# Cross-attention in split fp32r on one core: Q and K side by side, bv prefilled by ScalarE, two SBUF pools, a new order

## The chip, the cores and the metric

One core of a Trainium2 chip. The metric is the device time of one execution in microseconds (us). An execution's span runs from its first to its last profiled instruction; the time is a little longer than the span.

## The reference

For 8 batches, with x1 and x2 of 512 channels by 1024 positions in fp32 and D = 64:

```python
q = jnp.einsum('bcn,dc->bnd', x1, Wq) + bq
k = jnp.einsum('bcn,dc->bdn', x2, Wk) + bk[:, None]
v = jnp.einsum('bcn,dc->bdn', x2, Wv) + bv[:, None]
attn = jax.nn.softmax(jnp.einsum('bnd,bdm->bnm', q, k), axis=2)
attn_out = jnp.einsum('bcm,bnm->bcn', v, attn)
return attn_out + x1
```

Since the rows of attn sum to one, bv can be added behind the attention; the kernel does so, and writes the output transposed (position by channel).

## The kernel before

**The work of a batch.** Q and K are projected as plain fp32 matmuls of 64 columns (16 instructions each: 4 channel chunks, 2 halves of the positions, each in its own half of TensorE's columns). V, the scores and the output are products of fp32 operands, each split into a high part, a low part and a difference, and multiplied in three fp32r passes. The first two passes are accumulated in a PSUM bank, ScalarE scales the bank, and the third pass is added.

- V: 8 units j of 128 positions. VX(j) is the high and the low pass (4 matmuls each), vf(j) the scaling, VY(j) the third pass; vh, vl and vd split the result, ready for the output. The x2 chunks are split by xh (ScalarE), xl and xd (VectorE), one chunk for two units. In batch 0 units 0 and 1 are done by plain fp32 matmuls instead (VF).
- Scores: S(h, i), 2 matmuls for one half h of the rows and one block i of 128 columns; Sc copies them out of PSUM. Softmax goes by quarters Q of the rows: F and T find the maximum (T by GpSimd across partitions), and then by units u of 128 rows: L subtracts it (VectorE), E is exp (ScalarE), H, l and d make the three parts eh, el and ed (ScalarE, VectorE, VectorE). es, a1, a2, a3 and tot make the sum of a quarter (ScalarE, a DMA that accumulates, VectorE twice, GpSimd), few moves it by two small DMAs, rec inverts it.
- Output: R(u, m) is the high and low pass of unit u over block m of V, 2 matmuls; fx(u) scales the bank; D(u, m) is the third pass, 1 matmul. lo(u) fills an output tile with bv by a broadcast DMA from DRAM, oa(u) adds x1T to it by a DMA that accumulates (issued by GpSimd), ev(u) adds the attention (VectorE), st(u) stores it. Unit 7 of the last batch is added and stored in two halves, ev/st and ew/sw.
- Q and K: Q and K are the matmuls, qe and ke take them out of PSUM with the bias (ScalarE, two instructions), qd and kc copy each half to the other 64 partitions by two DMAs, qr and kr make the high parts (ScalarE), ql and kl the low ones (VectorE).

**The order** is written out by hand: three strings of words, FIRST for batch 0, MIDDLE for batches 1 to 6, LAST for batch 7. A word names a method and its arguments; a + ahead of it means the next batch, a - the one before. follow (line 481) calls them one by one, and each engine executes its own instructions in that order, each waiting for its operands and for a free buffer. SyncE's queue holds the loads, lo, st, few, qd and kc, in that order too. In MIDDLE the next batch's Q and K are separated by other matmuls, and the loads of x1 stand ahead of Q, those of x2 between the two:

```python
VY.5 vl.2 H.3 vf.3 vh.5 a2.0 a3.0 vh.4 vl.4 VY.3 vf.6 +ldx1.0 +Q vl.5 vh.3 T.2 l.3 F.3 VY.6 VX.7 tot.0 +qe R.0.0
...
H.4 l.4 +K E.5 es.2 vh.7 vl.7 R.0.7 +qd R.1.7 oa.1 +qr l.2 +ql vd.3 +ke fx.1 R.4.0 R.3.6 R.3.7 few.0 fx.3 R.4.1
```

In FIRST, batch 0's own K and Q follow one another on TensorE.

**Buffers.** Tiles of one tag rotate through as many buffers as BUFS gives it (one where it says nothing); a new tile waits until the tile that had the buffer is no longer read. kh, kl and kd hold both the parts of x2 (xh, xl, xd) and those of the exponentials (H, l, d); x holds the loads of x1 and x2; o the output tiles. q and k of a batch share one buffer (tag qk). In PSUM, tag B (5 banks) holds the units of V and of the output, tag sc (3 banks) Q, K and the scores.

Of the kernel before, what the change touches and what calls it, by code (L numbers as in the profile page):

```python
# [9 lines left out]
F32 = mybir.dt.float32  # L10
# [4 lines left out]

# [3 lines left out]

FIRST = """  # L30
VF.0.0 VF.0.1 VF.1.0 VF.1.1 ldx2.0 lwq VF.0.2 ldx2.1 wh.0 wl.0 VF.1.2 wd.0 VF.1.3 wh.1 ldx1.0 w4.0 wl.1 xh.1
w4.1 VF.0.3 vf.0 xl.1 VX.2 vh.0 vf.1 xh.3 vh.1 K ldx1.1 ke kc lo.0 vf.2 wd.1 Q xh.2 vl.0 qe xl.3 xd.1 VY.2 vh.2
xl.2 VX.4 xd.3 vl.1 qd VX.5 vd.0 kr vf.4 vf.5 qr kl VX.3 +ldx1.0 vf.3 xd.2 VY.4 vh.4 VY.5 lo.1 ql vl.2 VY.3
S.0.2 vh.5 S.0.0 vh.3 S.0.5 S.0.1 vl.4 S.0.3 vl.5 Sc.0.2 S.1.5 S.0.4 vd.2 Sc.0.0 Sc.0.5 Sc.0.1 Sc.0.3 S.0.6 vl.3
S.0.7 S.1.7 Sc.0.4 S.1.0 Sc.0.6 Sc.0.7 +ldx1.1 F.0 S.1.6 S.1.1 Sc.1.1 oa.1 VX.7 T.0 vd.1 L.0 Sc.1.5 vf.7 Sc.1.7
E.0 L.1 +Q E.1 VX.6 F.1 T.1 VY.7 S.1.3 H.0 l.0 Sc.1.0 R.0.0 S.1.2 Sc.1.6 es.0 H.1 S.1.4 Sc.1.3 +ldx2.0 L.2 +qe
vf.6 R.0.1 R.0.2 L.3 R.0.3 R.0.4 vh.7 +ldx2.1 VY.6 Sc.1.2 Sc.1.4 a1.0 l.1 R.1.0 R.1.1 R.1.2 E.3 d.0 R.1.3 R.1.4
R.1.5 R.0.5 F.2 vl.7 vh.6 H.3 +K l.3 R.3.0 T.2 d.1 vl.6 a2.0 +qd R.0.6 R.1.6 oa.0 E.2 R.3.1 R.3.2 R.3.3 R.3.4
R.3.5 R.3.6 R.0.7 H.2 l.2 +qr L.4 es.1 R.2.0 R.2.1 R.2.2 R.2.3 R.2.4 fx.0 a1.1 E.4 F.3 H.4 D.0.0 R.3.7 a3.0
R.2.5 d.3 R.2.6 R.2.7 l.4 fx.3 D.3.0 R.1.7 R.4.0 T.3 lo.3 D.0.1 D.0.2 fx.2 +ql L.6 E.6 lo.2 D.3.1 D.3.2 D.3.3  # L40
D.3.4 D.3.5 R.4.1 R.4.2 +ke a2.1 d.2 R.4.3 R.4.4 R.4.5 tot.0 vd.3 few.0 R.4.6 L.5 fx.1 D.0.3 D.0.4 D.2.0 D.0.5
D.0.6 H.6 D.2.1 D.2.2 D.0.7 +kc l.6 +xh.0 rec.0 E.5 R.4.7 a3.1 D.1.0 D.1.1 D.1.2 D.1.3 D.1.4 D.1.5 D.1.6 D.2.3
es.2 oa.2 H.5 ev.0 L.7 fx.4 E.7 d.4 st.0 D.1.7 R.6.0 D.2.4 D.3.6 tot.1 ev.1 R.6.1 R.6.2 R.6.3 R.6.4 R.6.5 R.6.6
+kr l.5 a1.2 +xl.0 R.5.0 D.2.5 D.4.0 R.5.1 D.3.7 R.6.7 D.2.6 few.1 H.7 +xh.1 R.5.2 R.5.3 D.4.1 d.6 es.3 oa.3
R.5.4 +kl +S.0.7 d.5 fx.6 +Sc.0.7 +S.0.5 R.5.5 D.2.7 st.1 D.6.0 +S.0.6 +Sc.0.5 a2.2 +xh.3 a3.2 +Sc.0.6 +S.0.3
a1.3 +S.0.2 R.5.6 lo.4 +Sc.0.3 +Sc.0.2 rec.1 ev.2 st.2 ev.3 st.3 +S.0.0 R.5.7 +S.0.1 l.7 D.4.2 +Sc.0.0 +xl.1
D.6.1 D.4.3 +S.0.4 +xd.0 tot.2 +VX.1 D.4.4 +Sc.0.4 +vf.1 +Sc.0.1 D.6.2 few.2 a2.3 lo.5 +F.0 a3.3 D.6.3 +S.1.6
lo.7 D.4.5 +Sc.1.6 rec.2 D.4.6 D.4.7 oa.4 d.7 +VX.0 ev.4 fx.5 D.5.0 D.5.1 D.6.4 D.6.5 +S.1.3 +vf.0 +VY.0 D.6.6
D.5.2 D.5.3 D.6.7 +xh.2 +T.0 R.7.0 lo.6 +L.1 +xl.3 R.7.1 tot.3 few.3 +L.0 +xd.1 oa.6 +F.1 rec.3 +Sc.1.3 oa.5
+E.1 +S.1.4 +H.1 oa.7 R.7.2 R.7.3 R.7.4 R.7.5 R.7.6 st.4 R.7.7 fx.7 +VY.1 D.7.0 D.7.1 D.7.2 +S.1.5 ev.6 +vh.1  # L50
+Sc.1.4 +xl.2 +E.0 D.7.3 D.7.4 D.7.5 D.5.4 D.5.5 D.5.6 D.5.7 ev.5 +vh.0
"""
# [40 lines left out]
def kernel(  # L93
# [41 lines left out]
    def new(shape, tag, name, dtype=F32):  # L135
        return sb.tile(shape, dtype, tag=tag, name=name, bufs=BUFS.get(tag, 1))

# [355 lines left out]


_OUT = (8, 1024, 512)


# [26 lines left out]
```

## Time and profile before

| | |
|---|---|
| Median of 3 runs | 655.53 us (655.47 to 656.39) |
| The profiled execution, its time | 656.37 us |
| its span | 654.6 us |
| TensorE busy | 648.5 us |
| VectorE busy | 563.3 us |
| ScalarE busy | 400.2 us |
| GpSimd busy | 195.3 us |
| Bytes moved by DMA | 106.73 MB, 163 GB/s in the mean |

Engines are named as the profile names them: PE is TensorE's matmuls, PEld its weight loads, DVE VectorE, ACT ScalarE, POOL GpSimd, SP SyncE; a q behind the name means its instruction queue, as where it issues a DMA. L418 is line 418 of the kernel. A row of a group reads: line, engine, operation, output<-inputs, shapes, xcount | busy us, mean ns of one | idle time of the engine just ahead of them, and what ended most of it. Matmuls are pipelined: one's duration is longer than the distance to the next one's start, and the distance is what it costs.

### The profile page before, as it was taken

The page shows a single profiled execution, that of the slowest core. Times are in us where ns is not written, and L with a number is a line of the kernel's source. Part 1 is how long each engine was busy: PE and PEld are TensorE (multiplying, and loading weights), DVE is VectorE, ACT ScalarE, POOL GpSimd, SP SyncE. Part 2 cuts the span into 40 slices and gives each one's busy share as a digit, 9 for nine tenths or more (in the row PEclk, how much of TensorE's full clock was granted, in tenths as well). Part 3 has the DMA queues.
Part 4 walks back from the last instruction along what each step waited for, and adds up shares of the span by engine and source line. Part 5 has one row for each costly group of instructions (what it writes and reads, how often), then busy time and mean ns, then how long its engine had stood idle before and what let it go on. Part 6 is the DMA issues. An engine that isn't in the chain of part 4 may idle for free.

```text
span 654.6 us, 7991 instructions
## 1 busy us (share of the span) xinstructions
PE 648.5 (99%) x2817; PEld 495.3 (76%) x2817; DVE 563.3 (86%) x661; ACT 400.2 (61%) x565; POOL 195.3 (30%) x164
## 2 busy tenths in 40 slices
PE   9999999999999999999999999999999999999997
PEld 4666788668886688866888668886688767888886
DVE  4789989997988979798897988979888798899982
ACT  5786857576466764767547674467645676467530
POOL 0023232324313333134231332313323133322513
PEclk9999999999999999999999999999999999999999
DMA  8645467594565855758557576676747676465466
GB/s 325 211 145 124 88 169 183 205 222 115 103 208 191 189 120 111 215 187 171 135 140 196 192 144 143 154 185 200 138 129 170 168 227 126 117 145 125 76 167 161
DMA packets 50552, 106.73 MB, mean 163 GB/s; under 512 B 14160, under 2 KB 14928, under 8 KB 46800
## 3 DMA queue, kind: packets, MB, share of 16 engines
q1 hardware_dynamic: 35968, 72.14, 34.6%
q0 software_dynamic: 13824, 33.56, 29.4%
q10 hardware_dynamic: 720, 0.53, 0.2%
q8 instruction: 22, 0.36, 0.2%
q14 instruction: 18, 0.15, 0.1%
HBM read 68.42 MB, written 16.78 MB: 130 GB/s over the span
## 4 chain that ended last, share of the span: by engine, by line
PE 86%; DMA 1%; DVE 1%; issue 0%; ACT 0%; DVEq 0%
PE ps_o L418 49%; PE ps_v L379 22%; PE ps_s L262 8%; PE ps_q L205 3%; PE ps_k L205 3%; DMA x<-in_x_dram 1%; DVE o L447 0%; DVE e L290 0%; DVE el L301 0%; ACT vh L401 0%; ACT ps_v L390 0%; DVEq L520 0%; DVE es L319 0%; DVE ed L306 0%
## 5 line engine op out<-in xcount | busy, mean ns | idle before, releaser
L418 PE MATMUL ps_o<-vh,eh 128*128 128x512 f32 x512 | 200.2, 391 | 0.0
L418 PE MATMUL ps_o<-vl,el 128*128 128x512 f32 x512 | 199.4, 390 | 0.3 <-DVE el L301 0.3
L418 PE MATMUL ps_o<-vd,ed 128*128 128x512 f32 x512 | 139.2, 389 | 0.0
L418 PEld LDWEIGHTS ps_o<-vh,eh 128*128 128x128 f32 x512 | 96.1, 188 | 25.9 <-issue 5.7
L418 PEld LDWEIGHTS ps_o<-vl,el 128*128 128x128 f32 x512 | 96.2, 188 | 20.4 <-DVE el L301 0.7
L418 PEld LDWEIGHTS ps_o<-vd,ed 128*128 128x128 f32 x512 | 96.0, 188 | 20.1 <-ACT ps_o L430 0.2
L329 POOL PARTITION_ALL_REDUCE den<-es x32 | 72.4, 2263 | 105.6 <-DVE es L319 94.1
L267 ACT COPY e<-ps_s 128x512 f32<-128x512 f32 x128 | 70.1, 593 | 49.5 <-PE ps_s L262 49.1
L440 POOL DMA_DIRECT2D o<-in_x1T_dram x64 | 58.2, 1006 | 134.7 <-DMA o<-in_bv_dram 53.6
L290 DVE TENSOR_TENSOR e<-e,top 128x1024 f32<-128x1024 f32 x64 | 88.7, 1388 | 7.7 <-POOL top L282 7.7
L282 POOL PARTITION_ALL_REDUCE top<-max x32 | 44.6, 1395 | 154.5 <-DVE max L278 106.3
L297 ACT ACTIVATE eh<-e 128x1024 fp32r<-128x1024 f32 x64 | 67.6, 1057 | 24.3 <-PE ps_o L418 23.7
L301 DVE TENSOR_TENSOR el<-e,eh 128x1024 fp32r<-128x1024 f32 x64 | 79.4, 1241 | 0.5 <-ACT eh L297 0.3
L306 DVE SCALAR_TENSOR_TENSOR ed<-eh,el 128x1024 fp32r<-128x1024 f32 x64 | 78.1, 1229 | 0.3
L293 ACT ACTIVATE e<-e 128x1024 f32<-128x1024 f32 x64 | 66.8, 1053 | 8.0 <-DVE e L290 7.8
L379 PE MATMUL ps_v<-wh,xh 128*128 128x512 f32 x248 | 66.9, 391 | 0.0
L379 PE MATMUL ps_v<-wl,xl 128*128 128x512 f32 x248 | 66.3, 389 | 0.0
L379 PE MATMUL ps_v<-wd,xd 128*128 128x512 f32 x248 | 64.7, 396 | 0.0
L447 DVE SCALAR_TENSOR_TENSOR o<-ps_o,r,o 128x512 f32<-128x512 f32 (+1 forms) x65 | 47.7, 739 | 18.7 <-PE ps_o L418 15.9
L390 ACT ACTIVATE ps_v<-ps_v 128x512 f32<-128x512 f32 x64 | 37.7, 589 | 40.8 <-PE ps_v L379 39.6
L379 PEld LDWEIGHTS ps_v<-wd,xd 128*128 128x128 f32 x248 | 44.9, 188 | 16.7 <-issue 4.9
L401 ACT ACTIVATE vh<-ps_v 128x512 fp32r<-128x512 f32 x64 | 37.5, 596 | 32.5 <-PE ps_v L379 32.2
(45 smaller groups left out, 815.8 us busy)
## 6 DMA issues: line engine op xcount, KB each, us to landing
x<-in_x_dram SPq DMA_DIRECT2D x29, 1024.0 KB, 7.2
o<-in_bv_dram SPq DMA_DIRECT2D x64, 256.0 KB, 4.5
o<-in_x1T_dram POOLq DMA_DIRECT2D x64, 256.0 KB, 4.6
es<-e POOLq DMA_DIRECT2D x32, 512.0 KB, 6.9
out_dram<-o SPq DMA_DIRECT2D x63, 256.0 KB, 4.0
x<-in_x_dram SPq DMA_DIRECT2D x5, 512.0 KB, 8.9
k<-k SPq DMA_DIRECT2D x16, 128.0 KB, 4.4
q<-q SPq DMA_DIRECT2D x16, 128.0 KB, 9.8
```

What stands on the lines that cost most here:

```text
L262: nc.tensor.matmul(ps, k[:, ts(i, P)], self.qa[:, ts(h, H)], start=(z == 0), stop=(z == 1))
L267: nc.scalar.copy(self.half[h][:, :, i, :], self.ps[h, i].rearrange("p (q n) -> p q n", q=2))
L290: nc.vector.tensor_tensor(e, e, top, ALU.subtract)
L293: nc.scalar.activation(self.unit(u), self.unit(u), AF.Exp)
L297: nc.scalar.activation(self.e[u]["h"], self.unit(u), AF.Copy, scale=SPLIT)
L301: nc.vector.tensor_tensor(self.e[u]["l"], self.unit(u), f32(self.e[u]["h"]), ALU.subtract)
L306: nc.vector.scalar_tensor_tensor(e["d"], f32(e["h"]), -1.0 / T, f32(e["l"]), ALU.mult, ALU.add)
L329: nc.gpsimd.partition_all_reduce(self.den[Q], self.es[Q][:, 0, :], P, ReduceOp.add)
L379: nc.tensor.matmul(self.B[j], self.c[j // 2][z][:, c, ts(j % 2, P)], w[z][:, c, :], start=(start and c == 0), stop=(stop and c == CT - 1), ...
L418: nc.tensor.matmul(self.B[u], self.e[u][z][:, m, :], self.v[m // 2, z][:, m % 2, :], start=start, stop=stop, skip_group_check=True,)
L440: nc.gpsimd.dma_start(self.o[u], x1T[self.b, ts(u, P), :], accum_op=ALU.add)
L447: nc.vector.scalar_tensor_tensor(o, self.B[u][:, at], self.share(u), o, ALU.mult, ALU.add)
```

## The change

- The words of the three orders are rearranged throughout. The next batch's Q and K follow one another on TensorE, with all four loads of x ahead of them, and x has 4 buffers instead of 2.
- VX is divided into XH and XL, two words that can stand apart.
- lo is a copy by ScalarE from bv_sb, a tile that is loaded once by one broadcast DMA (lbv).
- kh, kl, kd and o have one buffer less each. A second SBUF pool, side, holds the tags named in SIDE.
- At the start: the first piece of x2 is issued by SyncE instead of ScalarE, the bias load by SyncE later (lbq), and there are 8 warm-up matmuls instead of 9.
- At the end: the last unit in the order is unit 5. The halves of unit 7 remain, and sw is issued by ScalarE's queue.

The code, and of the orders the lines around Q and K in MIDDLE and the end of LAST:

```diff
 MIDDLE = """
...
+VY.7 vl.4 +ldx2.1 vf.3 -st.7 +Q +qe +K lo.2 L.7 E.7 l.1 H.0 F.2 vh.7 VY.3 VY.6 tot.0 a2.1 vh.3 l.0 vl.3 R.2.0
+R.0.0 vl.7 R.2.1 T.2 L.4 R.2.2 R.2.3 R.1.0 R.1.1 R.2.4 L.5 R.0.1 R.1.2 vd.0 R.2.5 lo.1 +qd +qr vh.6 R.3.0 R.3.1
+a3.1 few.0 lo.0 vl.6 E.5 +ql oa.2 E.4 +ke d.1 es.2 R.0.2 R.2.6 R.2.7 fx.2 R.3.2 R.3.3 R.3.4 R.0.3 R.0.4 d.2 vd.1
...
 LAST = """
...
+L.5 oa.0 -st.7 E.5 fx.0 d.0 R.3.5 R.2.5 L.4 a1.3 R.2.6 R.2.7 H.1 fx.2 oa.2 R.3.6 vd.2 R.3.7 E.4 D.0.0 es.2 D.2.0
...
+D.4.6 oa.5 d.6 D.4.7 oa.6 fx.6 D.6.0 D.6.1 ev.4 st.4 D.6.2 D.6.3 D.6.4 D.6.5 D.6.6 D.6.7 D.5.0 D.5.1 D.5.2 D.5.3
+ev.6 st.6 D.5.4 D.5.5 D.5.6 D.5.7 ev.5 st.5
 """
...
+    side = ctx.enter_context(tc.tile_pool(name="side", bufs=1))
...
+    bv_sb = const.tile([P, C], F32, name="bv_sb")
...
-    BUFS = {"B": 5, "sc": 3, "raw": 2, "top": 2, "kh": 5, "kl": 5, "kd": 4, "es": 2, "few": 2, "r": 2, "o": 4, "x": 2}
+    BUFS = {"B": 5, "sc": 3, "raw": 2, "top": 2, "kh": 4, "kl": 4, "kd": 3, "es": 2, "few": 2, "r": 2, "o": 3, "x": 4}
...
+    SIDE = {"raw", "o", "es", "qk", "fold", "top", "den", "few", "r"}
...
-        return sb.tile(shape, dtype, tag=tag, name=name, bufs=BUFS.get(tag, 1))
+        pool = side if tag in SIDE else sb
+        return pool.tile(shape, dtype, tag=tag, name=name, bufs=BUFS.get(tag, 1))
...
-            nc.scalar.dma_start(self.x2[0][:, 0, c, :], x2[0, :, 0, c])
+            queue = nc.scalar if c else nc.sync
+            queue.dma_start(self.x2[0][:, 0, c, :], x2[0, :, 0, c])
...
+        def lbq(self):
+            nc.sync.dma_start(bqk_sb, bqk)
+
+        def lbv(self):
+            nc.sync.dma_start(bv_sb, bv.broadcast_to([P, C]))
...
-        def VX(self, j):
+        def XH(self, j):
             self.B[j] = bank("B", f"ps_v_{self.b}_{j}")
             self.vpass(j, "h", True, False)
+
+        def XL(self, j):
             self.vpass(j, "l", False, True)
...
-            nc.sync.dma_start(self.o[u], bv.broadcast_to([P, C]))
+            nc.scalar.copy(self.o[u], bv_sb)
...
-            nc.sync.dma_start(outT[self.b, ts(u, P), right], self.o[u][:, right])
+            nc.scalar.dma_start(outT[self.b, ts(u, P), right], self.o[u][:, right])
...
-        nc.scalar.dma_start(bqk_sb, bqk)
...
-        for i, times in enumerate((3, 3, 3)):
+        for i, times in enumerate((3, 3, 2)):
```

103 lines of the change are left out of this document (49 added, 54 removed).

## The prediction

> **What bounds the kernel now.** I read the page of the profile first, then the busy time by stretches, then the waits. Three rows of the page, and two stretches of 80 us out of the middle:
>
> ```profile
> span 654.6 us, 7991 instructions
> PE 648.5 (99%) x2817; PEld 495.3 (76%) x2817; DVE 563.3 (86%) x661; ACT 400.2 (61%) x565; POOL 195.3 (30%) x164
> PE 86%; DMA 1%; DVE 1%; issue 0%; ACT 0%; DVEq 0%
> ```
>
> ```profile
> 180.00:260.00 80.00, 80.00 (x352) 61.70 (x352) 69.81 (x83) 49.39 (x70) 24.46 (x20) 1.00 0.64 163
> 260.00:340.00 80.00, 80.00 (x352) 61.69 (x352) 69.80 (x83) 49.38 (x70) 24.41 (x20) 1.00 0.66 165
> ```
>
> The columns after the stretch are the busy time of PE, PEld, DVE, ACT and POOL, the granted clock and the DMA share. TensorE is busy all of each 80 us, at full clock, and the chain that ended last runs through it. The change removes no matmul outside the warm-up: both orders hold the same projections, scores and outputs. So it can save only what TensorE loses between matmuls, and what lies ahead of its first and behind its last one. It can cost whatever makes TensorE wait. VectorE has about 10 us to spare in 80, ScalarE 30.
>
> What is lost between matmuls inside a batch is seen in TensorE's own timeline around a K projection in the middle, and around K and Q of the first batch, where they already stand side by side:
>
> ```profile
> 298.19 0.39 PE L418 MATMUL ps_o<-vh,eh 128*128 128x512 f32 x1
> 298.41 0.39 PE L418 MATMUL ps_o<-vl,el 128*128 128x512 f32 x1
> 298.73 3.65 PE L205 MATMUL ps_k<-x,wqk_sb 128*64 128x512 f32 x16
> 302.31 0.50 PE L418 MATMUL ps_o<-vh,eh 128*128 128x512 f32 x1
> 302.65 0.40 PE L418 MATMUL ps_o<-vl,el 128*128 128x512 f32 x1
> 302.89 0.39 PE L418 MATMUL ps_o<-vh,eh 128*128 128x512 f32 x1
> ```
>
> ```profile
> 14.19 3.65 PE L205 MATMUL ps_k<-x,wqk_sb 128*64 128x512 f32 x16
> ...
> 17.68 3.60 PE L205 MATMUL ps_q<-x,wqk_sb 128*64 128x512 f32 x16
> ...
> 21.21 1.20 PE L379 MATMUL ps_v<-wd,xd 128*128 128x512 f32 x4
> ```
>
> Durations overlap, so I read starts. Ordinary matmuls start every 0.22 to 0.23 us (298.19 to 298.41). Into the K block it takes 0.32 (298.41 to 298.73), 0.09 too much; behind it 0.34 (302.31 to 302.65), 0.11 too much. The block alone takes 3.58 (298.73 to 302.31); the joined pair of the first batch takes 14.19 to 21.21, 7.02, or 3.51 each, so a lone block loses 0.07 inside as well. Two lone blocks against one joined pair: one entry and one exit less, 0.20, and 7.16 less 7.02, 0.14. That is **0.34 us a batch**.
>
> The waits that reach TensorE, in the list of waits (total, times, longest):
>
> ```profile
> PEld ps_q L205 <- DMA x<-in_x_dram: 1.4, 1, 1.4
> PE ps_q L205 <- DMA x<-in_x_dram: 1.0, 1, 1.0
> PEld ps_v L372 <- DMA x<-in_x_dram: 0.8, 2, 0.5
> PEld ps_o L418 <- DVE el L301: 0.7, 1, 0.7
> PE ps_o L418 <- DVE el L301: 0.3, 1, 0.3
> ```
>
> Once each, in the first 125 us: a Q that waits 1.0 for its load, 0.3 to 0.7 for an el, 0.8 in two pieces for the first loads.
>
> **The change, part by part.**
>
> *Q and K side by side.* Batches 1 to 7 are projected in lone blocks, batch 0 already jointly: 7 x 0.34 = **-2.4 us**. Only the diff's word order is needed for this (+Q +qe +K, with nothing of TensorE between). Their inputs need four x buffers at once instead of two. In a middle batch the four loads now stand at its head; the buffers they take were last read by the previous pair and by xl.3 early in this batch, so they leave some 14 us ahead of Q, by the count of matmuls between. The 1.0 us wait of Q in batch 1 goes the same way, since in the first batch two loads find fresh buffers: **-1.0**.
>
> *bv by ScalarE.*
>
> ```profile
> o<-in_bv_dram SPq DMA_DIRECT2D x40, 256.0 KB, 4.7
> q<-q SPq DMA_DIRECT2D x10, 128.0 KB, 9.9
> k<-k SPq DMA_DIRECT2D x10, 128.0 KB, 4.5
> ```
>
> ```profile
> L312 ACT COPY es<-e 128x1024 f32<-128x1024 f32 x32 | 33.5, 1047 | 0.7
> L390 ACT ACTIVATE ps_v<-ps_v 128x512 f32<-128x512 f32 x64 | 37.7, 589 | 40.8 <-PE ps_v L379 39.6 <-ACT e L267 0.8 <-PE ps_v L372 0.4
> ```
>
> The first fence is the transfers issued from 180 to 580 us (times, size, median to landing). 64 broadcasts of 256 KB leave the SP queue, one of 256 KB (lbv) comes; TensorE waited for none, so I cost the removal at 0. ScalarE gets 64 copies of 128x512 from SBUF to SBUF, which no row shows. Bounds: 0.52 us, half the 1047 ns of the copy twice as wide, and 1.05, all of it; I take 0.6, the row of equal width (589). That is 8 x 0.6 = 4.8 us a batch, on 49.4 busy of 80; hidden in ScalarE's idle time, but each copy stands in order ahead of others. It also waits there for the store that frees its buffer (3 instead of 4); I follow the tightest place below.
>
> *Fewer split buffers (kh, kl, kd each one less) and the new order.* I followed each reuse in a middle batch by counting matmuls at 0.227. Most are free well before, and two places are thin, both behind Q and K. First, ScalarE does qe, lo.2, E.7, H.0 and VectorE l.0, from the end of Q. The durations are in these rows:
>
> ```profile
> L297 ACT ACTIVATE eh<-e 128x1024 fp32r<-128x1024 f32 x64 | 67.6, 1057 | 24.3 <-PE ps_o L418 23.7
> L293 ACT ACTIVATE e<-e 128x1024 f32<-128x1024 f32 x64 | 66.8, 1053 | 8.0 <-DVE e L290 7.8
> L301 DVE TENSOR_TENSOR el<-e,eh 128x1024 fp32r<-128x1024 f32 x64 | 79.4, 1241 | 0.5 <-ACT eh L297 0.3
> L290 DVE TENSOR_TENSOR e<-e,top 128x1024 f32<-128x1024 f32 x64 | 88.7, 1388 | 7.7 <-POOL top L282 7.7
> L405 DVE SCALAR_TENSOR_TENSOR vl<-vh,ps_v 128x512 fp32r<-128x512 f32 x64 | 42.5, 682 | 12.8 <-ACT vh L401 12.5
> L409 DVE TENSOR_TENSOR vd<-vh,vl 128x1024 fp32r<-128x1024 f32 x32 | 39.0, 1219 | 0.3
> L319 DVE TENSOR_TENSOR es<-es 128x256 f32<-128x256 f32 x32 | 13.3, 417 | 0.3
> L212 ACT ACTIVATE q<-ps_q,bqk_sb 64x512 f32<-64x512 f32 x16 | 11.0, 684 | 16.2 <-PE ps_q L205 16.0
> ```
>
> 1.37 + 0.6 + 1.05 + 1.06 + 1.24 = 5.3, and I allow 0.2 for hand-overs. TensorE asks for l.0 after K (3.5), VY.3 and VY.6 (8 matmuls) and 3 more: 6.0. It fits by 0.5. Behind l.0 VectorE does vl.3, vl.7, L.4, L.5, vd.0, a3.1, vl.6: 0.68 + 0.68 + 1.39 + 1.39 + 1.22 + 0.42 + 0.68 = 6.5, so vl.6 is there at 12.0; TensorE asks for it in R.2.6, 37 matmuls behind K, at 3.5 + 8.4 = 11.9. So this just misses, by 0.1: 6 middle batches, **+0.6**. In the last batch ScalarE does E.5, fx.0, H.1 and then fx.2, 1.05 + 0.6 + 1.06 + 0.6 = 3.3, behind an L.5 that VectorE, full until then, ends about 2.8 us ahead of the first D.2: **+0.5**. The wait for el in the first batch (0.3 to 0.7) belongs to an order that is gone; I take **-0.5**.
>
> *The start.*
>
> ```profile
> 0.98 4.02 PE L473 MATMUL ps_warm<-warm 128*128 128x512 bf16 x9 [0.98 <-DVE spark L468]
> ...
> 4.80 7.62 PE L372 MATMUL ps_v<-w_raw,x 128*128 128x512 f32 x16
> ```
>
> One warm-up matmul less would end them 0.4 earlier (9 of them from 0.98 to 4.80), but the first weights now stand second in the SP queue, behind hx.0, so the first VF may start as late as now. VF goes through the chunks in the order of landing, two products on each, which lets the 0.8 of waits go. Bounds 0 and 1.2; I take **-0.4**. The bias load moves from ScalarE's queue to SP's, behind ldx2.1 and ahead of x1; it is asked for by ke, behind K, and moves x1 by 1 KB.
>
> *The end.*
>
> ```profile
> 650.78 0.88 DVE L447 SCALAR_TENSOR_TENSOR o<-ps_o,r,o 128x256 f32<-128x256 f32 x2 [0.92 <-PE ps_o L418]
> 651.72 0.38 SPq L460 DMA_DIRECT2D out_dram<-o  x1
> ```
>
> ```profile
> out_dram<-o SPq DMA_DIRECT2D x3, 256.0 KB, 2.3
> out_dram<-o SPq DMA_DIRECT2D x2, 128.0 KB, 1.8
> L447 DVE SCALAR_TENSOR_TENSOR o<-ps_o,r,o 128x512 f32<-128x512 f32 x63 | 46.8, 747 | 17.8 <-PE ps_o L418 14.9 <-DMA o<-in_x1T_dram 1.8
> ```
>
> Now unit 7 comes last, in two halves: 0.88 of VectorE, then a store of 128 KB that lands in 1.8. The new order ends with unit 5, whole: 0.75, then 256 KB in 2.3. That is 0.5 - 0.13, **+0.4**. The halves of unit 7 and sw.7 on ScalarE's queue are some 14 us from the end. [...]
>
> **Sum:** -2.4 - 1.0 - 0.5 - 0.4 + 0.4 + 0.6 + 0.5 = -2.8. The profiled execution took 656.37 (span 654.6 and 1.8 around it), so 653.6; the median of the runs shown is 655.53, 0.84 less, so **652.7**. Without the two new waits and with all of the start it would be 650.8.
>
> **Rivals.**
>
> *The gains are eaten by thin chains.* If a bv copy takes 1.05 instead of 0.6, H.0, l.0 and vl.6 are each 0.45 later, and R.2.6 waits 0.55: 6 x 0.45 = 2.7 more, 655.4, no change. For it: no row shows the copy, and the chain has no slack. Against it: ScalarE's rows go by width, 589 at 512 and 1047 at 1024.
>
> *Slower: the copy of q holds up the v of unit 6.* In the new order qr, which waits for q's two copies, stands ahead of vh.6 on ScalarE; vl.6, and R.2.6, wait for that. From the end of Q: qe 1.37, copy, qr 1.06, vh.6 0.6, vl.6 0.68. With the 4.5 of k's copy it comes to 8.2 against the 11.9 at which R.2.6 asks; with the 9.9 that q's takes now, to 13.6, 1.7 too late, in 6 batches 10.2: 662.9. It decides from a copy of 8.2 us on. For it: 9.9 is the median now. Against it: now two loads of 1 MB are issued right ahead of q's copy, on the same queue; in the new order the loads stand a third of a batch earlier unless xl.3 or a store's wait on SP holds the last one back.
>
> *It doesn't do what it says:* Q and K adjacent in the order, but K waiting for x2 or for its bank. The bank was read out by Sc.1.6 long before; a late load of a microsecond in each batch would cost 7 x 1.0, 659.7.
>
> **How the numbers follow.** A measurement of this kernel can tell about 0.2%, 1.3 us, from no change. My forecast (650.6 to 654.2) gets 0.62, the thin chains 0.20, q's copy 0.12, a late load or a place that I didn't count 0.06. Faster 0.64 (the forecast and a little of the thin chains), same 0.17, slower 0.19. The range takes in the forecast and the thin chains, 0.82: 650.6 to 657.0.
>
> **What would show it.** In the timeline a period between Q blocks of about 79.9 to 80.0 instead of 80.2, with ps_q and ps_k adjacent; no wait of ps_q for x; ACT copies of o from bv_sb at about 600 ns; q's copy landing in under 6 us; the last store whole. If TensorE shows waits for vl or el in every batch, a thin chain decides; if ScalarE's qa waits more than 2 us for q, the second rival. I am wrong if the period is longer than 80.2.

## The result and the profile after

| | before | after |
|---|---|---|
| Median of 4 runs each | 655.78 us (655.47 to 656.39) | 660.10 us (659.38 to 661.46) |
| Ratio | | 1.0067 (95% interval 1.0049 to 1.0085) |
| The profiled execution, its time | 656.37 us | 661.46 us |
| its span | 654.6 us | 659.7 us |

The change made the kernel slower by 0.67%, where 652.7 us was forecast. Of the six executions of the run e8 below, two lie over 1.5% above its fastest one and are left out of its median, range and ratio. The page of the profile after, the same two stretches of 80 us as before, and TensorE's timeline around one joined pair:

```profile
span 659.7 us, 8029 instructions
...
PE 650.4 (99%) x2816; PEld 496.3 (75%) x2816; DVE 557.0 (84%) x661; ACT 433.8 (66%) x629; POOL 198.6 (30%) x164
```

```profile
180.00:260.00 80.00, 79.78 (x350) 61.13 (x349) 68.03 (x81) 52.74 (x77) 23.76 (x21) 1.00 0.57 139
260.00:340.00 80.00, 80.00 (x354) 62.18 (x353) 70.84 (x85) 53.65 (x79) 25.01 (x21) 1.00 0.55 138
```

```profile
205.74 1.07 PE L369 MATMUL ps_v<-wd,xd 128*128 128x512 f32 x4
206.74 3.65 PE L201 MATMUL ps_q<-x,wqk_sb 128*64 128x512 f32 x16
210.22 3.60 PE L201 MATMUL ps_k<-x,wqk_sb 128*64 128x512 f32 x16
213.76 0.50 PE L369 MATMUL ps_v<-wd,xd 128*128 128x512 f32 x1
```

The joined pair takes 206.74 to 213.76, 7.02 us, as the pair of the first batch took before. The gain is there. The stretch from 180 to 260 us no longer fills TensorE, though. The list of all waits says what it waits for. PEld rows are the weight load ahead of a matmul. Before, VectorE's first two rows came to 7.8 us in 2 waits and 1.8 us in 2, and no wait of a matmul itself (PE) came more than once:

```profile
DVE r L330 <- DMA few<-den: 25.8, 13, 3.1
DVE o L437 <- DMA o<-in_x1T_dram: 25.4, 6, 5.6
...
PEld ps_v L369 <- DVE o L437: 5.3, 5, 2.0
...
PE ps_v L369 <- DVE o L437: 3.2, 3, 1.6
...
PEld ps_o L408 <- ACT e L261: 1.7, 4, 0.4
...
PEld ps_s L256 <- DVE kl L251: 1.6, 3, 0.6
```

TensorE has three new waits (for DVE o, DVE kl and the one listed under ACT e), each in several batches. I follow the longest. TensorE, VectorE, and the transfers issued from 180 to 580 us:

```profile
436.05 1.98 PE L369 MATMUL ps_v<-wd,xd 128*128 128x512 f32 x8
439.31 1.20 PE L369 MATMUL ps_v<-wh,xh 128*128 128x512 f32 x4 [1.29 <-DVE o L437]
```

```profile
431.71 1.23 DVE L352 SCALAR_TENSOR_TENSOR xd<-xl,xh 128x1024 fp32r<-128x1024 f32 x1 [0.48 <-PE ps_o L408]
438.51 0.75 DVE L437 SCALAR_TENSOR_TENSOR o<-ps_o,r,o 128x512 f32<-128x512 f32 x1 [5.57 <-DMA o<-in_x1T_dram]
```

```profile
x<-in_x_dram SPq DMA_DIRECT2D x20, 1024.0 KB, 11.9
...
o<-in_x1T_dram POOLq DMA_DIRECT2D x40, 256.0 KB, 5.0
...
q<-q SPq DMA_DIRECT2D x10, 128.0 KB, 2.3
k<-k SPq DMA_DIRECT2D x10, 128.0 KB, 5.1
few<-den SPq DMA_DIRECT2D x40, 0.5 KB, 3.4
```

XH.4, the first pass of V's unit 4 (439.31), waits for a PSUM bank. That bank held the previous batch's output unit 7 until -ev.7 had read it (438.51), and ev.7, in VectorE's fixed order, sat idle 5.57 us for oa.7, the transfer that adds x1T to the output tile. Oa.7 was issued at 427.37 and landed 11.1 us later, while the median of its kind is 5.0; before, oa.7 took 4.4 to 5.4 us in batches 1 to 6, and 9.3 in batch 0. In that time the four loads of x, which the change put at the head of the batch, are under way, two to four of them at any moment. The stretch around it, with the one before and the one behind (columns as above, the last two the DMA share and GB/s):

```profile
410.00:424.00 14.00, 14.00 (x64) 11.59 (x63) 13.90 (x17) 10.89 (x16) 6.17 (x5) 1.00 0.39 95
424.00:440.00 16.00, 14.71 (x65) 11.75 (x64) 9.86 (x12) 10.48 (x17) 2.62 (x3) 1.00 0.99 294
440.00:450.00 10.00, 10.00 (x46) 7.78 (x45) 9.89 (x14) 6.74 (x10) 2.97 (x2) 1.00 0.62 187
```

A DMA share of 0.99: the 16 engines are busy nearly all of these 16 us, beside 0.39 just ahead of them. The start-to-start excess of TensorE there sums up to 3.9 us in four batches, with 0.11 us behind each wait.

The second wait: S.0.6, the next batch's first score, waits for kl (0.27 to 0.30 us, three batches, 0.11 behind each). VectorE at that place:

```profile
229.90 1.21 DVE L295 TENSOR_TENSOR el<-e,eh 128x1024 fp32r<-128x1024 f32 x1
232.73 0.17 DVE L330 RECIPROCAL r<-few 128x2 f32<-128x2 f32 x1 [1.62 <-DMA few<-den]
232.84 1.23 DVE L251 TENSOR_TENSOR kl<-k,kh 128x1024 fp32r<-128x1024 f32 x1
233.98 1.22 DVE L300 SCALAR_TENSOR_TENSOR ed<-eh,el 128x1024 fp32r<-128x1024 f32 x1
```

kl's input kh was there at 230.6. But the order has rec.1 ahead of kl, and rec.1 waits 1.62 us for few.1's transfers of 0.5 KB. These took 4.6 and 7.0 us here, issued right behind k's two copies and beside two oa and an es (DMA share 1.01 and 1.09 in the two stretches of 3 us from 225 us on); before, issued over 6 us behind k's copies, they took 2.9 and 3.7.

The third: D.3.0 waits (0.13 to 0.20 us in five batches, 0.08 behind each).

```profile
235.31 0.19 PEld L408 LDWEIGHTS ps_o<-vd,ed 128*128 128x128 f32 x1 [0.42 <-ACT e L261]
```

The row puts the wait down to a copy of scores (ACT e), which happened to end last in four of the five batches. But D.3.0 doesn't read those. Of its inputs, fx.3 had ended 0.46 to 0.94 us ahead of this weight load, and d.3, the row of 233.98 above, ends 0.115 us ahead of it in all five. So D.3.0 waits for d.3, which stands behind rec.1 and kl on VectorE: the third wait hangs on the same instruction as the second (but for the fifth batch, where kl waits for kh). The experiments below were set up in the belief that it was fx.3. Together these are 3.9 + 0.5 + 0.9 + 0.3 + 0.9 + 0.4 = 6.9 us.

The start was also later. TensorE there in the kernel after, and in a later run with the same start (kl and D.3, below):

```profile
0.98 3.60 PE L462 MATMUL ps_warm<-warm 128*128 128x512 bf16 x8 [0.98 <-DVE spark L457]
5.33 9.61 PE L362 MATMUL ps_v<-w_raw,x 128*128 128x512 f32 x16 [0.75 <-DMA w_raw<-in_wvT_dram]
```

```profile
5.22 7.11 PE L362 MATMUL ps_v<-w_raw,x 128*128 128x512 f32 x16 [0.64 <-DMA w_raw<-in_wvT_dram]
```

The weights come 0.75 us behind the last warm-up, and the 16 VF records take 9.61 us instead of the 7.62 of before: the first six distances are 0.75 to 0.99 us, about twice the 0.43 of the rest. VF's last record starts at 14.34 us, before at 11.82: 2.5 us. The second fence shows that this need not be.

### The profile page after: what moved, and what is told of

The parts are those of the page before. It is cut to its first block, busy times and chain, and to the rows that moved or that the text cites. A ratio compares the mean times of both kernels' runs of the same rounds, so it can differ in the third digit from the quotient of the medians.

```text
span 659.7 us, 8029 instructions
## 1 busy us (share of the span) xinstructions
PE 650.4 (99%) x2816; PEld 496.3 (75%) x2816; DVE 557.0 (84%) x661; ACT 433.8 (66%) x629; POOL 198.6 (30%) x164
## 4 chain that ended last, share of the span: by engine, by line
PE 54%; DMA 9%; DVE 4%; issue 3%; ACT 2%; SPq 0%; POOL 0%; POOLq 0%; ACTq 0%; DVEq 0%
PE ps_o L408 30%; PE ps_v L369 15%; DMA o<-in_x1T_dram 6%; PE ps_s L256 5%; PE ps_q L201 3%; DMA few<-den 2%; PE ps_k L201 2%; DVE e L284 1%; DVE o L437 1%; DMA out_dram<-o 1%; DVE vl L397 1%; DVE qa L234 1%; ACT k L208 0%; ACT q L208 0%; DVE kl L251 0%
## 5 line engine op out<-in xcount | busy, mean ns | idle before, releaser
L408 PE MATMUL ps_o<-vd,ed 128*128 128x512 f32 x512 | 143.0, 391 | 0.1
L321 POOL PARTITION_ALL_REDUCE den<-es x32 | 75.5, 2359 | 172.9 <-DVE es L311 155.5
L420 ACT ACTIVATE ps_o<-ps_o 128x512 f32<-128x512 f32 x64 | 37.1, 582 | 89.1 <-PE ps_o L408 88.8
L295 DVE TENSOR_TENSOR el<-e,eh 128x1024 fp32r<-128x1024 f32 x64 | 81.4, 1271 | 11.8 <-ACT eh L291 11.0
L276 POOL PARTITION_ALL_REDUCE top<-max x32 | 41.2, 1289 | 158.5 <-DVE max L272 158.5
L261 ACT COPY e<-ps_s 128x512 f32<-128x512 f32 x128 | 72.5, 593 | 19.2 <-PE ps_s L256 19.1
L284 DVE TENSOR_TENSOR e<-e,top 128x1024 f32<-128x1024 f32 x64 | 77.2, 1224 | 2.0 <-POOL top L276 1.9
L437 DVE SCALAR_TENSOR_TENSOR o<-ps_o,r,o 128x512 f32<-128x512 f32 (+1 forms) x65 | 47.9, 739 | 35.3 <-DMA o<-in_x1T_dram 25.4
L430 POOL DMA_DIRECT2D o<-in_x1T_dram x64 | 60.4, 1021 | 46.2 <-ACT o L427 40.9
L369 PE MATMUL ps_v<-wl,xl 128*128 128x512 f32 x248 | 64.5, 390 | 0.0
L369 PEld LDWEIGHTS ps_v<-wh,xh 128*128 128x128 f32 x248 | 46.1, 188 | 15.2 <-DVE o L437 5.3
```

Of the source, the lines that this page charges most:

```text
L261: nc.scalar.copy(self.half[h][:, :, i, :], self.ps[h, i].rearrange("p (q n) -> p q n", q=2))
L276: nc.gpsimd.partition_all_reduce(self.top[Q], self.fold[Q][:, 0, :], P, ReduceOp.max)
L284: nc.vector.tensor_tensor(e, e, top, ALU.subtract)
L295: nc.vector.tensor_tensor(self.e[u]["l"], self.unit(u), f32(self.e[u]["h"]), ALU.subtract)
L321: nc.gpsimd.partition_all_reduce(self.den[Q], self.es[Q][:, 0, :], P, ReduceOp.add)
L369: nc.tensor.matmul(self.B[j], self.c[j // 2][z][:, c, ts(j % 2, P)], w[z][:, c, :], start=(start and c == 0), stop=(stop and c == CT - 1), ...
```

## The experiments

All ratios are to the kernel before on the same chip. Lines of the orders are cut to the words that change. The numbers e1 to e18 are those of the runs in the order in which they were made.

**The start.** Theory A: the wait behind too few warm-ups leaves TensorE at half rate. Rival: the weights' landing alone counts.

```diff
-        for i, times in enumerate((3, 3, 2)):
+        for i, times in enumerate((3, 3, 3)):   # e1; e2: (4, 4, 4); e4: (3, 3, 2) in the kernel before
-            queue = nc.scalar if c else nc.sync
+            queue = nc.scalar                   # e3, with (3, 3, 2)
```

> The kernel after, with nine warm-up matmuls (3, 3, 3) as the kernel before has, and nothing else changed. In the kernel after the eight warm-ups end at 4.58 us, the first VF record begins at 5.33 us, the first six VF records stand 0.853 us apart and the rest 0.427, and VF ends at 14.34 us (before: 11.82). Theory A (TensorE comes to its full rate only after a stretch of work that is long and unbroken enough, and eight warm-ups with 0.75 us of idle time behind them are too little): the ninth ends at 5.0 us, the idle time shrinks to 0.3 us, most of the half-rate records go, VF ends at 12.2 to 13.0 us and the whole comes out 1.3 to 2.1 us shorter, about 658.5 us. Rival (only the later landing of the first weights counts, the half rate has another cause): VF still ends at 14.3 us, 660.1 us.

Measured: 660.15 us (656.81 to 661.31), 1.0055 (1.0035 to 1.0075). VF's last record started at 11.91 us with no half-rate gap but the first (0.64), 2.4 us earlier than in the profile of the kernel after, and yet the time didn't move.

> The kernel after with twelve warm-up matmuls (4, 4, 4), so that they reach past the landing of the first weights at 5.2 us. Theory A: the warm-ups end at 5.5 us (if the last ones already run at full rate) to 6.1 us (if none does), VF follows them without idle time with its records 0.427 us apart from the first, and ends at 12.4 to 13.0 us; the whole is 1.3 to 1.9 us shorter, 658.2 to 658.8 us. Rival (the half rate belongs to the VF matmuls or their operands, whatever ran ahead): the first VF records keep 0.853 us, VF ends at 14.5 us or later and the time is 660.1 us or more.

658.87 us (657.60 to 661.51), 1.0047 (1.0029 to 1.0065). The distance between warm-ups fell from 0.43 to 0.22 us from the eighth on, at 3.84 us; VF from 5.67 with one gap above 0.43 (0.51), last record 12.19.

> The kernel after with the very first x load back on ScalarE's queue, so that the first weights are first in SyncE's queue again; eight warm-ups as in the kernel after. The first weights land at 4.0 us and x at about 4.1 us, ahead of the end of the warm-ups at 4.58 us. If the idle time of 0.75 us ahead of VF is what costs the rate: VF follows at 4.6 us, its records 0.427 us apart, and ends at 11.6 to 11.9 us, the whole 2.5 us shorter, 657.6 us. If the number of warm-ups is what costs it (eight are one too few in any case): VF begins at 4.6 us with one to four records at 0.853 us and ends at 12.0 to 13.3 us, 1.0 to 2.3 us shorter. Rival (later landing alone, half rate from elsewhere): VF ends 0.7 us earlier than now, at 13.6 us, 659.4 us.

658.48 us (656.14 to 659.77), 1.0035 (1.0020 to 1.0051). VF from 4.37; two gaps above 0.43 (0.90, 0.70), last record 11.54.

> The kernel before with eight warm-up matmuls (3, 3, 2) instead of nine, and nothing else changed. Its first weights land at 4.01 us and VF begins at 4.80 us, behind the ninth warm-up. If only idle time ahead of VF costs the rate: VF begins at 4.4 us, stays at 0.427 us from record to record and ends at 11.4 to 11.8 us, 655.4 to 655.8 us. If nine warm-ups are needed whatever follows: the first one to four VF records stand 0.853 us apart, VF ends at 11.8 to 13.2 us and the time rises by 0 to 1.4 us, to 655.8 to 657.2 us.

655.65 us (655.08 to 657.69), 1.0001 (0.9990 to 1.0011): no difference; three gaps above 0.43 (0.53, 0.74, 0.53), last record 11.26.

The traces of the start answer better than the times. Ten of the runs below have the start of the kernel after unchanged. In seven of their profiles VF's last record started at 11.74 to 12.08 us, in three at 13.5 to 13.9. So the 2.5 us of the profile after are what this start does in 4 of 11 profiles; its usual price is about 0.1 us (11.9 beside 11.8). Theory A holds in part: with more warm-ups or earlier weights no profile has more than three slow gaps at the head of VF, and none ends VF later than 12.2 us. But eight warm-ups with the same wait behind them often did as well, so their number alone isn't the cause.

The clock records show how the late starts differ, and not why. In the profile after the first record of full clock begins at 10.36 us, at the end of the half-rate records. By the records of all eleven profiles with this start it begins at 3.9 to 5.1 us in the seven good ones, ahead of VF, and at 8.8 to 10.4 us in the four others. The length of the wait behind the warm-ups doesn't tell them apart: it is 0.75 us in the profile after, 0.64 in that of e7, whose 16 VF records take 7.11 us, and 1.3 in that of e11, where the idle times between VF's weight loads, the longest left out, are 0.24 us in the mean, as at the full rate (0.52 at half). In the other starts it is at most 0.3 us (0.26 in e1), or, in e2, 0.59 us behind warm-ups that already stood 0.22 us apart. The same eight warm-ups of 3.6 us were followed by 0 to 6 half-rate records, and what decides between them isn't shown.

**The order of VectorE and of D.3.0 (theory C/D).**

```diff
-few.1 D.2.6 rec.1 +kl d.3
+few.1 D.2.6 +kl rec.1 d.3
-ev.2 D.3.0 +S.0.3 +Sc.0.2 D.0.0 D.0.1 +Sc.0.3 D.3.1
+ev.2 +S.0.3 +Sc.0.2 D.0.0 D.0.1 +Sc.0.3 D.3.0 D.3.1
```

> The kernel after with two places of the middle batches' order changed: kl ahead of rec.1 on VectorE (rec.1 waits for the small transfers of few.1, and kl, whose input has been there for 1.7 us, stands behind it), and D.3.0 behind D.0.0 and D.0.1 (fx.3 has just begun when D.3.0 stands first). Theory C/D: the waits of S.0.6 for kl (0.27 to 0.30 us in three batches, with 0.11 us of weight load behind each) and of D.3.0 for fx.3 (0.13 to 0.20 in five batches, with 0.08) go, about 2.3 us in all; 657.8 us. Rival (S.0.6 is held by the copy of k on ScalarE, late behind ql): the waits ahead of S.0.6 stay, only D's 1.3 us go, 658.8 us.

656.46 us (653.46 to 659.40, 12 runs), 1.0012 (0.9994 to 1.0029): 3.6 us less than the kernel after. No wait for kl, and none of D.3.0, is left. The only large one:

```profile
PE ps_v L369 <- DVE o L437: 2.3, 1, 2.3
```

It is in the second batch, and it costs more than its length, as the stretch behind it shows (the column ahead of the last two is the granted clock):

```profile
114.20:117.00 2.80, 2.80 (x8) 2.20 (x7) 2.70 (x6) 0.00 (x0) 0.00 (x0) 0.51 1.05 301
```

Half clock for some 3 us behind a stall of 2.3: 1.4 us more. The same is in the profile of e1, the longest of its six executions (2.23 us, then a granted clock of 0.50 from 114.8 to 118 us): that stall with the half clock behind it costs about 4 us there, 1.9 at the same place in the kernel after, which takes back most of the 2.4 us of the better start.

**x1's loads out of the head (theory B).** x1's buffers are free from the previous Q on, so their load can leave a batch earlier. A word with ++ means the batch after the next; FIRST takes +ldx1.1 ahead of +ldx2.0.

```diff
-E.3 +ldx1.1 S.1.7 VY.1        ...        XL.2 +ldx1.0 -ev.6
+E.3 S.1.7 VY.1                ...        XL.2 -ev.6
-R.1.3 +kc R.0.5
+R.1.3 +kc ++ldx1.0 ++ldx1.1 R.0.5
```

> The kernel after with the two 1 MB transfers of each batch's x1 taken out of the head of the batch and issued in the middle of the one before, right behind K's repeat transfers, into the two x buffers that Q has just read; the two x2 transfers stay at the head. 2 MB instead of 4 MB are then under way when the last x transfer into an output tile (oa.7) is. In the profile of the kernel after, the first pass of V's unit 4 waited in four batches, 3.9 us in all, for ev.7, which waited for oa.7 (9.6 to 11.1 us from issue to landing, median of all such transfers 4.7). Theory B (the four loads of the head delay oa.7, and through ev.7 hold the bank of V's unit 4): oa.7 lands in 5 to 8 us, the waits of unit 4 fall from 3.9 us to under 1.5 us, 657 to 658 us. Rival B1 (oa.7 is issued too late, whatever else runs): oa.7 still takes 9 us or more, the waits stay between 3 and 4.5 us, 660.1 us. Rival B2: the moved loads delay the small transfers of the middle (few, q and k repeat), and what unit 4 gains is lost ahead of the scores.

698.54 us (696.55 to 700.71), 1.0652 (1.0628 to 1.0676). XH.4 waits no more; rival B2 came true, far larger than I thought. Its waits:

```profile
PE ps_s L256 <- DVE kl L251: 32.5, 7, 7.0
```

```profile
DVE r L330 <- DMA few<-den: 47.4, 9, 8.4
```

few.1's 0.5 KB, issued 2 us behind two loads of 1 MB on the same queue, landed after 10.3 and 11.0 us (5.0 to 7.0 at that place in the kernel after). rec.1 waited for them, and kl stood behind rec.1. It is the chain of theory C made visible by stretching it.

> As the last, and the two x2 transfers issued behind the store of the last unit (st.7), so behind ev.7: no x load is under way when oa.7 is. Theory B: oa.7 lands in 4 to 6 us and the waits of V's unit 4 are 0 to 0.3 us; 2 MB are then on the way for 7 to 10 us and land just ahead of K, so that 655.5 to 656.5 us come out if K doesn't wait, and one to two us more if it does. Rival B1 (order alone): waits of unit 4 as now, 3 to 4.5 us, 660 us.

698.94 us (697.95 to 700.80), 1.0665 (1.0643 to 1.0686): the same stall. Next, both edits together:

> x1's transfers in the middle of the batch before (as in the run of x1 early) and kl ahead of rec.1, D.3.0 behind D.0.0 and D.0.1 (as in the run of kl and D.3) together. With x1 early alone, few.1's transfers of 0.5 KB stood behind two of 1 MB on SyncE's queue and took 10 us instead of 2, rec.1 waited for them, and kl, then S.0.6, stood 6 to 7 us behind rec.1 in each batch: 35 us. If that queueing on VectorE was the whole cause: with kl ahead of rec.1 those 35 us go, V's unit 4 waits not at all (in the run with kl and D.3 alone it still waited 2.5 us), and 653 to 654.5 us come out. If the late rec.1 now holds ev.2 and the banks behind it: waits of the output pass for a bank of one to several us a batch in its place, 656 to 670 us. If theory B is wrong: unit 4 waits about 2.5 us as in the run of kl and D.3, 656.5 us.

688.40 us (682.55 to 690.55), 1.0479 (1.0444 to 1.0513). S.0.6 is free but for one wait of 0.9 us, but d.3 still stands behind rec.1, and D.3.0 waits for it far longer than in the kernel after:

```profile
PE ps_o L408 <- DVE ed L300: 22.0, 5, 4.7
```

> As the last, with x2's transfers behind st.7 too. If only the burst at the head mattered, as the last (653 to 654.5 us); if the 2 MB of x2 land behind Q, K waits for them and the time is 1 us or more a batch above the last, 660 us.

686.75 us (685.11 to 690.22), 1.0471 (1.0444 to 1.0498): the same stall, and K doesn't wait for x2.

> As the run of x1 early with kl and D.3, with nine warm-ups and the first x load back on ScalarE's queue, so that the first weights are first on SyncE's. Weights land at 4.0 us, VF begins at 4.4 to 4.8 us behind the warm-ups. In five profiles with after's start VF ended at 11.7 to 14.3 us with the same instructions, in the four others at 11.3 to 12.2 us; so 0.4 us (weights) to 1.2 us (the mean of the half-rate records) less than the run beside it: 652 to 654 us. Rival (the start's records differ by chance alone): no difference to the run beside it beyond 0.4 us.

688.24 us (685.58 to 688.55), 1.0481 (1.0456 to 1.0505): the same stall; VF without a slow record.

> The kernel after with kl and D.3 as above and x1's two transfers of the batch after the next behind few.1 on SyncE's queue, where nothing is issued for 11 us in the profile of the kernel after (386.7 to 397.6 us). If the 29 to 40 us lost in the runs of x1 early came from few.1's transfers standing behind 2 MB (10 us instead of 2 to 6), few.1 lands in 2 to 6 us again and those stalls go; if theory B holds as well, V's unit 4 waits 0 to 0.3 us in all, against 2.5 us with kl and D.3 alone: 653 to 654.5 us. Rival (the loads in the middle of the batch slow a1.1, k's repeat or oa as well, whichever place they have): stalls of several us a batch stay, 660 us or more.

```diff
-few.1 D.2.6 rec.1 +kl d.3
+few.1 ++ldx1.0 ++ldx1.1 D.2.6 +kl rec.1 d.3
```

652.90 us (652.76 to 653.08), **0.9954** (0.9941 to 0.9967): 0.5% faster than before. Few.1's transfers now go ahead of the loads. The head of the batch, its oa.7 and VectorE's wait:

```profile
418.00:434.00 16.00, 16.00 (x72) 13.09 (x71) 11.76 (x16) 10.81 (x17) 3.37 (x4) 1.00 0.91 249
```

```profile
DVE o L437 <- DMA o<-in_x1T_dram: 2.8, 3, 1.4
```

The row of 25.4 us is down to 2.8, oa.7 lands in 5.1 to 6.8 us instead of 9.1 to 11.1, with one or two loads under way instead of two to four, and no XH.4 waits. The five runs agree within 0.3 us, where the kernel after spread over 2 us and e7 over 6. That it was the waits on transfers that varied is likely, but not shown: the start varies too.

> The kernel after with kl and D.3 as above and x1's two transfers behind the last unit's store (st.7) on SyncE's queue, so behind ev.7; x2's two stay at the head. They are issued at about 10 us into the batch and have some 13 us to Q. Theory B: oa.7 lands in 5 to 8 us instead of 8 to 11, unit 4 waits 0 to 0.5 us in all, 653.5 to 655 us. Rival B1 (oa.7 is issued too late whatever runs beside it): unit 4 waits 2 to 2.5 us as in the run with kl and D.3 alone, 656.5 us. If x1 lands late: Q waits by what it lacks.

```diff
-VY.7 vl.4 +ldx2.1 vf.3 -st.7 +Q
+VY.7 vl.4 +ldx2.1 vf.3 -st.7 +ldx1.1 +ldx1.0 +Q
```

661.41 us (658.69 to 664.08), 1.0086 (1.0063 to 1.0109). oa.7 landed in 4.2 to 5.0 us and XH.4 waits no more, but x1 came too late:

```profile
PE ps_q L201 <- DMA x<-in_x_dram: 5.8, 4, 3.4
```

So B1 (issued too late anyhow) falls in both runs, and the wait that the change took from Q (1.0 us) returns when the loads stand close ahead of it.

> The kernel after with x1's transfers behind few.1 and nothing else changed: rec.1 stays ahead of kl, D.3.0 ahead of D.0.0. Theory B alone: unit 4's waits (3.9 us and 0.55 us of weight load in the profile of the kernel after) go, those ahead of S.0.6 and D.3.0 (2.3 us) stay: 655.5 to 656.5 us. If the moved loads delay few.1's last transfer, rec.1 and with it kl are later than now and S.0.6 waits 0.5 us or more in each batch: 658 us or more.

658.41 us (654.97 to 662.73), 1.0037 (1.0015 to 1.0059). In its profile XH.4 doesn't wait and those of S.0.6 and D.3.0 stay (2.2 and 1.1 us, with what follows them). The median misses theory B's range by 2 us and lies in that of the second alternative, whose cause isn't there, though: few.1 takes 4.4 to 7.1 us in the middle batches, as in the kernel after, and S.0.6 waits 0.3 to 0.5 us in four of them. The late start of this profile (VF's last record at 13.87 us) is 2.1 us, the size of the miss; whether the other executions had it, and what spread them over 7.8 us, isn't shown. By the ratios theory B alone is worth about 2.0 us, kl and D.3 alone (e7) 3.6, both together (e13) 7.4.

> The kernel after with kl and D.3 as above, nine warm-ups and the first x load on ScalarE's queue; all x loads at the head as in the kernel after. Beside the run of kl and D.3 (656.5 us) 0.4 to 1.5 us less, 655 to 656 us, with V's unit 4 waiting 2 to 2.5 us as there; the run before it should be 1.5 to 2.5 us shorter than this one if theory B holds, and equal if not.

655.09 us (652.73 to 656.45), 0.9977 (0.9962 to 0.9991). XH.4 waited 3.1 us in two batches.

> As the last, with nine warm-ups and the first x load on ScalarE's queue. By the profiles VF ends at 11.3 to 11.9 us with the weights first in SyncE's queue and at 11.7 to 14.3 us without: 0.4 to 1.5 us less than the run before it, 652 to 654 us. If the half-rate records come by chance and as often here: within 0.4 us of it.

659.68 us (657.23 to 661.46), 1.0057 (1.0037 to 1.0077); Q waited for x1 as in e14.

> The run of x1 behind few.1 (652.9 us, with kl and D.3) with nine warm-ups and the first x load on ScalarE's queue. In that run's profile VF began at 5.2 us and had no half-rate record; the weights' earlier landing is worth 0.4 to 0.9 us there, and the half-rate records that three of ten profiles with the old start show go: 652.0 to 652.5 us. Rival (what follows VF waits for wh.0 and the x pieces anyway): 652.9 us.

**652.06 us** (651.62 to 652.98), 0.9942 (0.9929 to 0.9955), the fastest: by the medians the start is worth 0.8 us here, though the intervals of the two ratios overlap. The other two pairs (e7 and e16, e14 and e15) give 1.4 and 1.7.

**bv by transfers again.**

```diff
-            nc.scalar.copy(self.o[u], bv_sb)
+            nc.sync.dma_start(self.o[u], bv.broadcast_to([P, C]))
```

> The kernel after with the output tiles filled by the broadcast transfer of bv from DRAM again, on SyncE's queue at the same place of the order, instead of ScalarE's copy; the order, the pools and Q beside K stay. 64 transfers of 256 KB come back (90 MB become 107 MB) and ScalarE loses 64 copies of 0.61 us. If the copies of bv cost nothing and their transfers cost nothing (what the prediction says): 660.1 us. If the fewer transfers are worth something under the burst of loads at the head of the batch, lo.7 and oa.7 land later still and the waits of V's unit 4 grow from 3.9 us to 6 us or more: 662 to 666 us. If ScalarE's copies delay what stands behind them (fx.3, the copy of k): the waits of D.3.0 shrink and 659 us come out.

677.63 us (673.56 to 681.54, four executions), 1.0333 (1.0287 to 1.0379), 17.5 us more than the kernel after and above all three expectations. In the profile of the fastest execution V's unit 4 waits 6.8 us, as the second one said, and the last batch has waits of 1.5 to 3.8 us for el and ed that none named. SyncE's queue:

```profile
SPq L427 <- DMA out_dram<-o: 157.5, 46, 6.3
```

With three o buffers each broadcast waits for the store that frees its tile, and all that is behind it on SyncE's queue, few and the loads, waits too. So in this order the copy by ScalarE isn't neutral. That it is what makes three buffers enough is argued from this row, not shown: four buffers with the broadcasts were not tried.

**K apart from Q again**, in the middle batches.

```diff
-VY.7 vl.4 +ldx2.1 vf.3 -st.7 +Q +qe +K lo.2
+VY.7 vl.4 +ldx2.1 vf.3 -st.7 +Q +qe lo.2
-R.0.1 R.1.2 vd.0 R.2.5
+R.0.1 R.1.2 +K vd.0 R.2.5
```

> The kernel after with kl and D.3 as above, and K taken away from Q in the middle batches, between R.1.2 and R.2.5, so that each batch has two lone blocks of 64-column matmuls again. By the rows of before a lone block costs 0.34 us more (0.09 at the entry, 0.07 inside, 0.11 and 0.07 at the exit): six batches give 2.0 us, 658.5 us beside the 656.5 of the run of kl and D.3. Rival (side by side brings nothing, the entry and exit are paid elsewhere): 656.5 us and the sums of the gaps around the blocks as in the kernel after.

682.97 us (682.43 to 685.42), 1.0416 (1.0391 to 1.0440). Not the 2 us of a lone block, but this, in each batch:

```profile
129.62 0.39 PE L408 MATMUL ps_o<-vl,el 128*128 128x512 f32 x1
131.59 0.49 PE L408 MATMUL ps_o<-vh,eh 128*128 128x512 f32 x1 [1.59 <-ACT eh L291]
132.85 0.50 PE L408 MATMUL ps_o<-vl,el 128*128 128x512 f32 x1 [0.77 <-DVE el L295]
```

The block of K had covered the chain qe, lo.2, E.7, H.0, l.0. The block of Q ended at 127.4, and the matmul that waited for el.0 began at 132.85, 5.4 us later; the prediction had 5.3 for that chain. Behind the two waits seven matmuls stand 0.43 us apart instead of 0.23. The time of this run can't tell the lone block's price, but its trace can:

```profile
123.86 3.65 PE L201 MATMUL ps_q<-x,wqk_sb 128*64 128x512 f32 x16
127.44 2.11 PE L369 MATMUL ps_v<-wd,xd 128*128 128x512 f32 x8
```

Q alone takes 3.58, and so does K in each of the six batches, against 7.02 for the pair joined; with one entry (0.09) and one exit (0.11) more that is 0.35 us a batch, as forecast.

## Why the prediction was wrong, point by point

**Q and K joined: right.** Two starts of Q, four batches apart, in the kernel after's order without its stalls (e13), and before:

```profile
202.67 3.65 PE L201 MATMUL ps_q<-x,wqk_sb 128*64 128x512 f32 x16
```

```profile
522.08 3.23 PE L201 MATMUL ps_q<-x,wqk_sb 128*64 128x512 f32 x14
```

```profile
201.94 3.65 PE L205 MATMUL ps_q<-x,wqk_sb 128*64 128x512 f32 x16
```

```profile
522.90 3.65 PE L205 MATMUL ps_q<-x,wqk_sb 128*64 128x512 f32 x16
```

(522.08 - 202.67) / 4 = 79.85 us, before 80.24: 0.39 us a batch, where 0.34 was forecast (0.35 by the blocks alone, as in e11; the other 0.04 is not followed) and "79.9 to 80.0 instead of 80.2" named as the sign. In the kernel after it is (530.32 - 206.74) / 4 = 80.90. That, by the sign named, is the proof of error. Of its 1.05 us a batch above 79.85, the three waits in these four batches make 0.97.

**Q's wait for x, the copy by ScalarE, the copy of q: right.** The copy takes 0.62 us (the row below; 0.6 taken), q's two copies land in 2.3 us, so the rival of 8.2 us and more is out, and Q waits for no load.

```profile
L427 ACT COPY o<-bv_sb 128x512 f32<-128x512 f32 x64 | 39.4, 619 | 8.4 <-DMA out_dram<-o 4.0 <-DVE o L437 3.5 <-DVE max L269 0.5
```

**The thin chains (+0.6, +0.5): not there.** No matmul waits for vl.6 or for fx.2 in any profile of this order in which K is not moved. Both were sums that missed or met by 0.1 to 0.5 us.

**The end (+0.4): 0.0.** From the end of the last matmul (651.83 + 4.01 after) to that of the span it is 3.85 us, before (646.05 + 4.70) 3.82. The last store of 256 KB landed in 2.0 us, not 2.3.

```profile
651.83 4.01 PE L408 MATMUL ps_o<-vd,ed 128*128 128x512 f32 x17
```

```profile
646.05 4.70 PE L418 MATMUL ps_o<-vd,ed 128*128 128x512 f32 x20
```

**The start (-0.4): wrong in sign and in kind.** The bounds of 0 and -1.2 held no loss. It is about 0.1 us in seven profiles of eleven and 1.7 to 2.5 in the others; I counted the landing, and not that VF could begin at half rate (distances of 0.75 to 0.99 us instead of 0.43).

**The step that failed: "I followed each reuse in a middle batch ... Most are free well before."** I followed the reuse of the split buffers, and not that of the PSUM bank that unit 4 of V takes from unit 7 of the output. It hangs on ev.7, ev.7 on oa.7, and oa.7 is under way together with the four loads that "now stand at its head" (11.1 us to its landing instead of 5.0, at a DMA share of 0.99). I asked whether the loads come early enough for Q (they do: in the middle batches the last of x1 lands 6 to 11 us ahead of it), and not what they delay. The second rival saw loads ahead of a small transfer on one queue, but looked at q's copy alone. Nor did I read VectorE's order for an instruction that waits on a transfer (rec.1) ahead of two that TensorE needs (kl and d.3). These cost 6.9 us in the profile, and the start 2.5, against 2.7 for the joined pairs, 1.1 for Q's wait and 0.8 for the stalls of before that went (for el at 79 us, and one at 628 us): 5.1 is the difference of the spans, 4.8 the sum of these.

That e13 runs in 652.9 us, where 652.7 was forecast, is partly luck. The sum held 1.5 us of losses that never came (both thin chains and the end) and took each of the three gains 0.1 to 0.3 us too small. E13's trace has the gains of 2.7, 1.1 and 0.8 us above, and against them 1.3 us of other small waits between 97 and 112 us: 3.3 of the 3.4 us between its span (651.2) and that of before (654.6). So the gains were priced about right; what decided was what the change made late, which stood at nothing in the sum.

What stays open: how much of the 4.3 us between the medians is the start (0.1 to 2.5 us a run) and how much the transfers; e13, with the same start, says that about 7 us of the kernel after are waits, and slow starts where they came, that can be had back. Whether issuing oa.7 earlier, or keeping few.1 clear of k's copies, would do as well as moving the loads was not tried.

## What to carry to other kernels

When a change moves loads, don't ask only whether they arrive in time: list the transfers that will be under way beside them, and for each of these the instruction that waits for it, what stands behind that on its engine, and whose bank or tile it frees. On an engine with a fixed order, an instruction that waits for a transfer belongs behind those whose inputs are ready and that TensorE needs (here rec.1, which sat idle 1.62 us with kl's input there); and a small transfer that someone waits for belongs ahead of large ones on its queue (few.1 took 10.3 and 11.0 us behind two loads of 1 MB in e5, 5.0 to 7.0 at that place in the kernel after).

## What the runs showed of the hardware

- **TensorE's granted clock was half for some us behind some of its waits.** Behind the wait of 2.3 us ahead of XH.4 in e7 it was 0.51 from 114.2 to 117.0 us, behind 2.23 us in e1 0.50 from 114.8 to 118 us, and in e16, where the longest was 2.6 us, 0.50 from 114.2 to 116.6 us. In e11 it was 0.50 from 133.6 to 136.8 us, behind waits of 1.59 and 0.77 us within 3.3 us. Behind the wait of 1.58 us ahead of XH.4 in the second batch of the kernel after it stayed at 1.00 (116 to 120 us). From which wait on it happens isn't shown.
- **A printed clock of 1.00 stood where there is no record.** In the profile after, the stretch of half-rate VF records is printed with a clock of 1.00:

```profile
5.30:9.70 4.40, 4.37 (x5) 1.85 (x6) 1.78 (x2) 2.70 (x3) 0.00 (x0) 1.00 1.06 414
```

But the first clock record of this trace begins at 10.36 us, and the matmuls are at full rate from 10.48 on. Ahead of that record the distances between matmuls tell the rate, and the printed clock doesn't.

- **A transfer that accumulates took 4.2 to 5.0 us beside one load of 1 MB at a time (oa.7 in e14), 5.1 to 6.8 beside one or two (e13) and 9.1 to 11.1 beside two to four (the kernel after)**, though it was issued on GpSimd's queue and they on SyncE's.
